# Four graph-attention layers on one core: the row factor G by DMA and ScalarE copies in place of TensorE transposes, with normalisation, statistics and value copies moved between engines

## The chip, the cores and the metric

The kernel runs on one core of one Trainium2 chip. Its time is the device time of one execution in microseconds (us), the median over runs. A core has TensorE (PE, matrix products and transposes), VectorE (DVE), ScalarE (ACT), GpSimd (POOL), and SyncE (SP), which here only issues DMAs. Each engine works through its own queue; semaphores tie the queues together. SBUF is the on-chip memory of 128 partitions, PSUM the memory that TensorE writes.

## The reference

Input x has 16 batches of 1024 nodes with 256 features; one adjacency matrix of 1024 x 1024 serves all. Four layers follow, each `x = x + gat(relu(layernorm(x)))`. A layer has H heads of D = 256/H features, with H = 4, 1, 4, 1:

```python
Wh = h @ W                                  # 1024 x 256, per head 1024 x D
e  = leaky_relu(e_src[i] + e_dst[j])        # slope 0.2, in the last layer 0.01
e  = where(adj[i, j], e, -inf)
y  = softmax(e, over j) @ Wh                # per head
gat = elu(y)                                # in the last layer relu(y)
```

Layers 0 and 1 mask with adj > 0, layers 2 and 3 with adj != 0. `e_src` and `e_dst` are products of Wh with the two halves of the vector a.

## The kernel before

**The algebra.** exp(leaky_relu(s + d)) is the larger of two products of an i-factor and a j-factor. What depends on i alone cancels in the softmax, so that for every pair (j, i) the weight is `w = max(G[i], r[j]) * mask[j, i]`, with the remaining j-factor folded into the values. G[i] is `gcol` (L215, capped in L217), r[j] is `rcol` (L212), and the values `whx` carry the j-factor (L196) in a last column, so that one matrix product gives numerator and denominator.

**Tiling.** The 1024 nodes lie as C = 8 chunks of 128 partitions. A *tile* is the weight matrix of one chunk j against all 1024 i, 128 x 1024 float32 in SBUF, made by one VectorE operation (L236). Its input `g` is G of one head, the same row of 1024 numbers in all partitions, in PSUM. It is made by eight TensorE transposes of a column that is broadcast along the free axis (`broadcast`, L226 to L231); two `g` buffers exist. A four-head layer has 32 tiles, a one-head layer 8.

**Aggregation** (L240 to L256). TensorE multiplies each tile with the values, summing over the eight j. A *group* is what fills one accumulator: in a four-head layer four chunks i of one head (two groups a head), in a one-head layer one chunk i over 257 columns. Each layer has eight groups. ScalarE copies each accumulator to `y` (L256); there are two accumulators.

**Preparation** (L148 to L224). Statistics by VectorE (`stats`, L160, L161), the reciprocal root by GpSimd (L164, L165), the normalised rows by ScalarE (L174), per half of the nodes: four transposes for each 128 features by TensorE (L182), a relu copy by ScalarE (L183), then for each chunk the product with W (L194), an exponential (L196), the copy of the source and destination terms (L198) and the copy of the values: for one head with the factor as scale (L200), for four heads raw (L203), with the factor multiplied in by GpSimd (L205). `factors` ends it.

**Finish** (L258 to L304). Reciprocal of the denominators (L273, VectorE), then for each half a multiplication and a clamp by GpSimd (L277, L282), the exponential of ELU by ScalarE (L286), the combination by VectorE (L292) and the addition to x by GpSimd (L293). After the last layer L295 and the store L296 stand in place of these.

**Order.** 64 *steps* (a batch in a layer) run one after the other, numbered from 0. Four batches are in work at a time, so that a step's preparation and finish can be laid beside the groups of other steps. From step 3 on four-head and one-head steps mostly alternate; in cycles of eight steps the pattern of heads is 4 1 4 1 1 4 1 4. The main loop (L363 to L381) writes the order of all queues out by hand. Each group is a slot. In it stand: the tiles that the group needs; its products and its copy; the pieces of the last step's finish that are due; the pieces of preparations that are due (`prepare`); and some tiles ahead (four in a four-head step, two in a one-head step), no further than WBUFS tiles past what has been consumed. `PREPARATION` gives each piece's slot, counted from the group at which the step is planned: that is group 0 of the step two before, or group 4 where the batch's own last step is too near, as for steps 3, 5, 6, 8, 62 and 63. A tile can be written into the order only once its step's preparation is complete, and `emit_tiles` puts the head's `broadcast` in when the tiles are within half a head of it.

**Buffers.** 21 tiles w, three buffers `t4` shared by normalised rows and exponentials, two PSUM buffers `pp` for transposes and projections.

Of the kernel before, what the change touches and what calls it, by code (L numbers as in the profile page):

```python
# [33 lines left out]
P = 128  # L34
# [4 lines left out]
WBUFS = 21  # L39
PREPARATION = (0, 0, 1, 2, 3, 3, 4, 4, 5, 5, 5, 5, 6, 6, 7, 7, 8)  # L40
# [11 lines left out]
def kernel(ctx: ExitStack, tc: tile.TileContext, x, adj, ws, avs, out):  # L52
# [83 lines left out]
    ps_acc = ctx.enter_context(tc.tile_pool(name="ps_acc", bufs=2, space=PSUM))  # L136
    ps_p = ctx.enter_context(tc.tile_pool(name="ps_p", bufs=2, space=PSUM))
# [10 lines left out]
    def preparation(n):  # L148
# [6 lines left out]
        def stats(half):  # L155
# [6 lines left out]
            if half == 1:  # L162
# [3 lines left out]
                shift = st["shift"] = small.tile([P, C], F32, name="shift")  # L166
                nc.gpsimd.tensor_tensor(shift, st["mv"][:, :, 0], rstd, op=ALU.mult)
                nc.gpsimd.tensor_scalar(shift, shift, -1.0, None, op0=ALU.mult)

        def normalise(half):  # L170
            xn = st["xn", half] = prep.tile([P, HALF, F], F32, name="t4", bufs=3)
            for q in range(HALF):
                c = half * HALF + q
                nc.scalar.activation(xn[:, q, :], xs[b][:, c, :], AF.Identity,  # L174
                                     bias=st["shift"][:, c:c + 1], scale=st["rstd"][:, c:c + 1])
# [10 lines left out]
        def project(c):  # L186
# [12 lines left out]
            if H == 1:  # L199
                nc.scalar.activation(whx[:, c, 0, 0:D], pw[:, 0:D], AF.Copy,  # L200
                                     scale=whx[:, c, 0, D:D + 1])
            else:
                nc.scalar.activation(whx[:, c, :, 0:D],  # L203
                                     pw[:, 0:F].rearrange("p (h d) -> p h d", h=H), AF.Copy)
                nc.gpsimd.tensor_tensor(whx[:, c, :, 0:D], whx[:, c, :, 0:D],  # L205
                                        whx[:, c, :, D:D + 1].to_broadcast([P, H, D]),
                                        op=ALU.mult)
# [10 lines left out]

        out = [lambda: stats(0), lambda: stats(1), lambda: normalise(0), lambda: normalise(1)]
# [3 lines left out]

        return list(zip(PREPARATION, out + [factors], strict=True))  # L224

    def broadcast(n, h):  # L226

        g = state[n]["g", h] = ps_g.tile([P, N], F32, name="g")
        for c in range(C):
            nc.tensor.transpose(g[:, c * P:(c + 1) * P],  # L230
                                state[n]["gcol"][:, c, h:h + 1].to_broadcast([P, P]), ident)  # L231
# [26 lines left out]
    def finish(n):  # L258
# [16 lines left out]
        def scaled(half):  # L275
# [7 lines left out]

        def exponential(half):
# [135 lines left out]
```

## Time and profile before

| | before |
|---|---|
| median of 3 runs | 2823.59 us (2823.42 to 2825.28) |
| the profiled execution | 2825.28 us |
| its span, first to last instruction | 2823.2 us |
| granted TensorE clock, mean | 0.994 |
| busy PE / DVE / ACT / POOL | 2675.6 / 1986.5 / 1054.9 / 897.0 us |
| weight products L252 on PE | 1939.1 us |
| projections L194, transposes of rows L182, G transposes L230 | 509.1, 153.0, 169.6 us |
| tiles L236 on DVE | 1280 of 1273 ns |
| bytes moved by DMA | 45.60 MB |

Busy times are unions over the run; an instruction's own duration overlaps with the start of the next on the same engine, so that a row's sum can exceed what it takes from the queue. The view of the chain follows the last instruction back, at each step to what released it. In the groups, the last column is the idle time of the engine just before the group and what ended most of it. In the order of time the columns are start, duration, engine, line, operation, tiles and count, then the idle time ahead and its releaser. In the view by stretches each pair gives busy time and number of instructions for PE, weight loads (PEld), DVE, ACT and POOL, then the granted clock, the share of the DMA engines and GB/s.

### The profile page before, as it was taken

The page shows a single profiled execution, that of the slowest core. Times are in us where ns is not written, and L with a number is a line of the kernel's source. Part 1 is how long each engine was busy: PE and PEld are TensorE (multiplying, and loading weights), DVE is VectorE, ACT ScalarE, POOL GpSimd, SP SyncE. Part 2 cuts the span into 40 slices and gives each one's busy share as a digit, 9 for nine tenths or more (in the row PEclk, how much of TensorE's full clock was granted, in tenths as well). Part 3 has the DMA queues.
Part 4 walks back from the last instruction along what each step waited for, and adds up shares of the span by engine and source line. Part 5 has one row for each costly group of instructions (what it writes and reads, how often), then busy time and mean ns, then how long its engine had stood idle before and what let it go on. Part 6 is the DMA issues. An engine that isn't in the chain of part 4 may idle for free.

```text
span 2823.2 us, 90054 instructions
## 1 busy us (share of the span) xinstructions
PE 2675.6 (95%) x41296; PEld 2387.0 (85%) x41296; DVE 1986.5 (70%) x2569; ACT 1054.9 (37%) x3041; POOL 897.0 (32%) x909
## 2 busy tenths in 40 slices
PE   1899999999999999999999999999999999999998
PEld 1788888888988888888988889888898888888887
DVE  6597675576975678748777469667696577875672
ACT  0423424343333343343344343343333334344331
POOL 0233424233223244243242243333423324324221
PEclk9999999999999999999999999999999999999999
DMA  4000000000000000000100000000010000000000
GB/s 143 7 3 2 2 2 2 2 32 9 25 32 15 18 2 3 2 1 32 32 2 32 31 2 3 2 2 17 16 33 17 16 32 2 3 2 1 17 17 30
DMA packets 38842, 45.60 MB, mean 16 GB/s; under 512 B 3136, under 2 KB 37440, under 8 KB 38464
## 3 DMA queue, kind: packets, MB, share of 16 engines
q1 hardware_dynamic: 35776, 38.80, 4.1%
q8 instruction: 324, 5.31, 0.8%
q10 hardware_dynamic: 2688, 1.05, 0.1%
q14 instruction: 54, 0.44, 0.1%
HBM read 23.07 MB, written 16.78 MB: 14 GB/s over the span
## 4 chain that ended last, share of the span: by engine, by line
PE 89%; DVE 5%; ACT 3%; DMA 1%; POOL 1%; issue 1%; DVEq 0%; ACTq 0%; SPq 0%; POOLq 0%
PE acc L252 64%; PE pp L194 16%; PE g L230 5%; PE pp L182 4%; DVE w L236 3%; ACT whx L196 1%; ACT whx L200 1%; DMA a_bc<-in_L_gnn_a 1%; ACT y L256 1%; DVE bn L160 0%; ACT whx L203 0%; DVE mask L129 0%; POOL gcol L217 0%; DVE t L292 0%; DVE mv L161 0%
## 5 line engine op out<-in xcount | busy, mean ns | idle before, releaser
L252 PE MATMUL acc<-whx,w 128*64 128x65 f32 x36864 | 1939.1, 241 | 21.7 <-DVE w L236 21.6
L252 PEld LDWEIGHTS acc<-whx,w 128*64 128x64 f32 x36864 | 1749.9, 145 | 180.0 <-issue 41.1
L236 DVE SCALAR_TENSOR_TENSOR w<-g,rcol,mask 128x1024 f32<-128x1024 f32 x1280 | 1544.1, 1273 | 419.7 <-PE acc L252 249.5
L256 ACT ACTIVATE y<-acc 128x260 f32<-128x260 f32 (+1 forms) x512 | 197.8, 386 | 1433.0 <-PE acc L252 1433.0
L194 PE MATMUL pp<-wx,hT 128*128 128x258 f32 (+1 forms) x2048 | 509.1, 392 | 2.0 <-ACT hT L183 2.0
L277 POOL TENSOR_TENSOR y<-y,r 128x1024 f32<-128x1024 f32 x128 | 242.8, 1898 | 814.3 <-DVE r L273 814.3
L194 PEld LDWEIGHTS pp<-wx,hT 128*128 128x128 f32 x2048 | 379.4, 190 | 67.1 <-ACT hT L183 3.0
L205 POOL TENSOR_TENSOR whx<-whx 128x256 f32<-128x256 f32 x256 | 157.7, 617 | 599.0 <-ACT whx L203 599.0
L293 POOL TENSOR_TENSOR x<-x,t 128x1024 f32<-128x1024 f32 x96 | 227.2, 2366 | 227.2 <-DVE t L292 227.2
L174 ACT ACTIVATE t<-x,shift,rstd 128x256 f32<-128x256 f32 x512 | 265.2, 590 | 47.7 <-POOL x L293 42.5
L273 DVE RECIPROCAL r<-y 128x32 f32<-128x32 f32 (+1 forms) x64 | 17.7, 277 | 324.5 <-ACT y L256 324.5
L196 ACT ACTIVATE whx<-pp,nbias 128x4 f32<-128x4 f32 (+1 forms) x512 | 135.3, 264 | 192.0 <-PE pp L194 179.1
L230 PE MATMUL g<-ident,gcol 128*128 128x128 f32 x1280 | 169.6, 275 | 38.8 <-POOL gcol L217 38.8
L160 DVE BATCH_NORM_STATS2 bn<-x 128x6 f32<-128x256 f32 x512 | 200.7, 392 | 2.2 <-DMA x<-in_x 2.2
L230 PEld LDWEIGHTS g<-ident,gcol 128*128 128x128 f32 x1280 | 142.1, 137 | 59.4 <-POOL gcol L217 50.9
L182 PE MATMUL pp<-ident,t 128*128 128x128 f32 x1024 | 153.0, 282 | 27.8 <-ACT t L174 12.7
L182 PEld LDWEIGHTS pp<-ident,t 128*128 128x128 f32 x1024 | 110.9, 141 | 70.5 <-ACT whx L200 28.0
L183 ACT ACTIVATE hT<-pp 128x512 f32<-128x512 f32 x256 | 145.9, 595 | 20.7 <-PE pp L182 19.1
L292 DVE SCALAR_TENSOR_TENSOR t<-t,y 128x1024 f32<-128x1024 f32 x96 | 118.6, 1235 | 39.4 <-ACT t L286 39.4
L200 ACT ACTIVATE whx<-pp,whx 128x256 f32<-128x256 f32 x256 | 121.4, 474 | 0.0
L165 POOL TENSOR_TENSOR rstd<-rstd,neghalf 128x8 f32<-128x8 f32 x64 | 106.7, 1666 | 5.3
L161 DVE BATCH_NORM_AGGREGATE mv<-bn 128x2 f32<-128x6 f32 x512 | 92.8, 181 | 16.9
(35 smaller groups left out, 593.7 us busy)
## 6 DMA issues: line engine op xcount, KB each, us to landing
x<-in_x SPq DMA_DIRECT2D x16, 1024.0 KB, 5.3
out<-x SPq DMA_DIRECT2D x32, 512.0 KB, 3.1
a_raw<-in_adj SPq DMA_DIRECT2D x8, 512.0 KB, 3.7
a_bc<-in_L_gnn_a ACTq DMA_DIRECT2D x8, 128.0 KB, 5.9
wx<-in_L_gnn_W SPq DMA_DIRECT2D x4, 256.0 KB, 12.4
```

The source lines that it names most:

```text
L160: nc.vector.bn_stats(st["bn"][:, c, :], xs[b][:, c, :])
L174: nc.scalar.activation(xn[:, q, :], xs[b][:, c, :], AF.Identity, bias=st["shift"][:, c:c + 1], scale=st["rstd"][:, c:c + 1])
L182: nc.tensor.transpose(pt[:, q, :], st["xn", half][:, q, k * P:(k + 1) * P], ident)
L194: nc.tensor.matmul(pw, lhsT=st["hT", half][:, k, q * P:(q + 1) * P], rhs=wx[l][:, k, :], start=(k == 0), stop=(k == K - 1))
L196: nc.scalar.activation(whx[:, c, :, D], pw[:, F + H:F + 2 * H], AF.Exp, bias=nbias[l], scale=slope)
L205: nc.gpsimd.tensor_tensor(whx[:, c, :, 0:D], whx[:, c, :, 0:D], whx[:, c, :, D:D + 1].to_broadcast([P, H, D]), op=ALU.mult)
L230: nc.tensor.transpose(g[:, c * P:(c + 1) * P], state[n]["gcol"][:, c, h:h + 1].to_broadcast([P, P]), ident)
L236: nc.vector.scalar_tensor_tensor(w, state[n]["g", h], state[n]["rcol"][:, jc, h:h + 1], masks[LAYERS[steps[n][1]][3]][:, jc, :], op0=ALU.m ...
L252: nc.tensor.matmul(acc[o % P:o % P + cols, q, :], lhsT=st["w", h, jc][:, o:o + cols], rhs=st["whx"][:, jc, h, :], start=(jc == 0), stop=(j ...
L256: nc.scalar.activation(st["y"][:, i0:i0 + per, h, :], acc, AF.Copy)
L277: nc.gpsimd.tensor_tensor(yh, yh, r[:, :, None].to_broadcast([P, HALF * H, D]), op=ALU.mult)
L293: nc.gpsimd.tensor_add(xh, xh, e)
```

## The change

G reaches PSUM in another way. At the end of a preparation one transpose turns all of `gcol` into rows (C x H rows of 128), ScalarE copies them to SBUF (`gT`), and a DMA writes them to DRAM, one row of 1024 for each head (`rows`). For each head, `fetch` reads that row from DRAM into all 128 partitions of `gs` (two buffers), and `broadcast` becomes a ScalarE copy from `gs` to PSUM. `fetch_heads` issues fetches up to two heads ahead.

With it: rows are normalised by GpSimd (subtract and multiply in one operation) and not by ScalarE; four-head values are copied head by head by ScalarE with the factor as scale, and the GpSimd multiplication L205 is gone; the exponential of a half stands directly behind its GpSimd operations and no longer a slot later; `prepare` comes after the tiles of a slot; the slots of a preparation are spread from 0 to 10 and not 0 to 8; and there are 19 w buffers.

```diff
@@ -36,8 +36,8 @@
 SHIFT = 60.0
 EXP_SHIFT = math.exp(SHIFT)
 STREAMS = 4
-WBUFS = 21
-PREPARATION = (0, 0, 1, 2, 3, 3, 4, 4, 5, 5, 5, 5, 6, 6, 7, 7, 8)
+WBUFS = 19
+PREPARATION = (0, 1, 1, 1, 3, 3, 4, 4, 5, 5, 6, 6, 7, 7, 8, 8, 9, 10)
 
 
 LAYERS = [
@@ -134,6 +134,7 @@
     work = ctx.enter_context(tc.tile_pool(name="work", bufs=2))
     ps_g = ctx.enter_context(tc.tile_pool(name="ps_g", bufs=2, space=PSUM))
     ps_acc = ctx.enter_context(tc.tile_pool(name="ps_acc", bufs=2, space=PSUM))
+    dram = ctx.enter_context(tc.tile_pool(name="dram", bufs=4, space=bass.MemoryType.DRAM))
     ps_p = ctx.enter_context(tc.tile_pool(name="ps_p", bufs=2, space=PSUM))
 
     L = len(LAYERS)
@@ -163,16 +164,13 @@
                 rstd = st["rstd"] = small.tile([P, C], F32, name="rstd")
                 nc.gpsimd.tensor_scalar(rstd, st["mv"][:, :, 1], EPS, None, op0=ALU.add)
                 nc.gpsimd.tensor_tensor(rstd, rstd, neghalf, op=ALU.pow)
-                shift = st["shift"] = small.tile([P, C], F32, name="shift")
-                nc.gpsimd.tensor_tensor(shift, st["mv"][:, :, 0], rstd, op=ALU.mult)
-                nc.gpsimd.tensor_scalar(shift, shift, -1.0, None, op0=ALU.mult)
 
         def normalise(half):
             xn = st["xn", half] = prep.tile([P, HALF, F], F32, name="t4", bufs=3)
             for q in range(HALF):
                 c = half * HALF + q
-                nc.scalar.activation(xn[:, q, :], xs[b][:, c, :], AF.Identity,
-                                     bias=st["shift"][:, c:c + 1], scale=st["rstd"][:, c:c + 1])
+                nc.gpsimd.tensor_scalar(xn[:, q, :], xs[b][:, c, :], st["mv"][:, c, 0:1],
+                                        st["rstd"][:, c:c + 1], op0=ALU.subtract, op1=ALU.mult)
 
         def transpose(half, k):
             if k == 0:
@@ -196,15 +194,9 @@
             nc.scalar.activation(whx[:, c, :, D], pw[:, F + H:F + 2 * H], AF.Exp, bias=nbias[l],
                                  scale=slope)
             nc.scalar.activation(st["sd"][:, c, :], pw[:, F:F + 2 * H], AF.Copy)
-            if H == 1:
-                nc.scalar.activation(whx[:, c, 0, 0:D], pw[:, 0:D], AF.Copy,
-                                     scale=whx[:, c, 0, D:D + 1])
-            else:
-                nc.scalar.activation(whx[:, c, :, 0:D],
-                                     pw[:, 0:F].rearrange("p (h d) -> p h d", h=H), AF.Copy)
-                nc.gpsimd.tensor_tensor(whx[:, c, :, 0:D], whx[:, c, :, 0:D],
-                                        whx[:, c, :, D:D + 1].to_broadcast([P, H, D]),
-                                        op=ALU.mult)
+            for h in range(H):
+                nc.scalar.activation(whx[:, c, h, 0:D], pw[:, h * D:(h + 1) * D], AF.Copy,
+                                     scale=whx[:, c, h, D:D + 1])
 
         def factors():
             sd = st["sd"]
@@ -216,19 +208,32 @@
                                  scale=-(1.0 - slope))
             nc.gpsimd.tensor_scalar(gcol, gcol, EXP_SHIFT, None, op0=ALU.min)
 
+        def rows():
+
+            pt = ps_p.tile([C * H, P], F32, name="pp")
+            nc.tensor.transpose(pt, st["gcol"].rearrange("p c h -> p (c h)"), ident)
+            gT = small.tile([C * H, P], F32, name="gT", bufs=2)
+            nc.scalar.activation(gT, pt, AF.Copy)
+            st["grow"] = dram.tile([H, C, P], F32, name="grow")
+            nc.sync.dma_start(out=st["grow"].rearrange("h c i -> c h i"), in_=gT)
+
         out = [lambda: stats(0), lambda: stats(1), lambda: normalise(0), lambda: normalise(1)]
         for half in range(2):
             out += [lambda half=half, k=k: transpose(half, k) for k in range(K)]
             out += [lambda c=c: project(c) for c in range(half * HALF, (half + 1) * HALF)]
 
-        return list(zip(PREPARATION, out + [factors], strict=True))
+        return list(zip(PREPARATION, out + [factors, rows], strict=True))
+
+    def fetch(n, h):
+
+        gs = state[n]["gs", h] = work.tile([P, N], F32, name="gs", bufs=2)
+        nc.sync.dma_start(out=gs, in_=state[n]["grow"][h].rearrange("c i -> (c i)")
+                          .partition_broadcast(P))
 
     def broadcast(n, h):
 
         g = state[n]["g", h] = ps_g.tile([P, N], F32, name="g")
-        for c in range(C):
-            nc.tensor.transpose(g[:, c * P:(c + 1) * P],
-                                state[n]["gcol"][:, c, h:h + 1].to_broadcast([P, P]), ident)
+        nc.scalar.activation(g, state[n]["gs", h], AF.Copy)
 
     def weights(n, h, jc):
 
@@ -272,7 +277,7 @@
             st["r"] = small.tile([P, C, H], F32, name="r")
             nc.vector.reciprocal(st["r"], st["y"][:, :, :, D])
 
-        def scaled(half):
+        def exponential(half):
             xh, yh, r = views(half)
             nc.gpsimd.tensor_tensor(yh, yh, r[:, :, None].to_broadcast([P, HALF * H, D]),
                                     op=ALU.mult)
@@ -280,10 +285,7 @@
 
                 e = st["e", half] = prep.tile([P, HALF * H, D], F32, name="t4", bufs=3)
                 nc.gpsimd.tensor_scalar(e, yh, 0.0, -3.0e38, op0=ALU.min, op1=ALU.max)
-
-        def exponential(half):
-            if l < L - 1:
-                nc.scalar.activation(st["e", half], st["e", half], AF.Exp)
+                nc.scalar.activation(e, e, AF.Exp)
 
         def add(half):
             xh, yh, r = views(half)
@@ -299,8 +301,7 @@
             if half == 1 and b + STREAMS < B:
                 load(b + STREAMS)
 
-        return [(0, divide), (0, lambda: scaled(0)), (1, lambda: scaled(1)),
-                (1, lambda: exponential(0)), (2, lambda: exponential(1)),
+        return [(0, divide), (0, lambda: exponential(0)), (1, lambda: exponential(1)),
                 (2, lambda: add(0)), (3, lambda: add(1))]
 
 
@@ -314,7 +315,7 @@
     tiles = [(n, h, jc) for n, (b, l) in enumerate(steps) for h in range(LAYERS[l][0])
              for jc in range(C)]
     place = {t: i for i, t in enumerate(tiles)}
-    done = {"tiles": 0, "g": 0, "free": 0, "prepared": 0, "wanted": 0}
+    done = {"tiles": 0, "g": 0, "gs": 0, "free": 0, "prepared": 0, "wanted": 0}
     agenda = []
 
     def prepare(upto):
@@ -324,11 +325,21 @@
             piece()
             if last:
                 done["prepared"] = n + 1
+                fetch_heads()
 
     def plan(n, at):
         new = preparation(n)
         agenda.extend((at + k, n, piece, i == len(new) - 1) for i, (k, piece) in enumerate(new))
         agenda.sort(key=lambda a: a[:2])
+
+    def fetch_heads():
+
+        while done["gs"] < min(done["g"] + 2 * C, len(tiles)):
+            n, h, _ = tiles[done["gs"]]
+            if n >= done["prepared"]:
+                break
+            fetch(n, h)
+            done["gs"] += C
 
     def emit_tiles(upto, must=False):
         while done["tiles"] < min(upto, len(tiles)):
@@ -343,6 +354,7 @@
                     prepare(-1)
                 broadcast(n, h)
                 done["g"] += C
+                fetch_heads()
             if i >= done["g"]:
                 return
             weights(*tiles[i])
@@ -371,9 +383,9 @@
                     done["free"] = place[n, h, C - 1] + 1
                 while ending and ending[0][0] <= k:
                     ending.pop(0)[1]()
-                prepare(8 * n + k)
                 ahead = 4 if per > 1 else 2
                 emit_tiles(min(done["tiles"] + ahead, done["free"] + WBUFS))
+                prepare(8 * n + k)
             for _, piece in ending:
                 piece()
             ending = finish(n)
```

## The prediction

> **What bounds the kernel now.** I read the page from its top: busy shares, the chain that ended last, the groups.
>
> ```profile
> PE 2675.6 (95%) x41296; PEld 2387.0 (85%) x41296; DVE 1986.5 (70%) x2569; ACT 1054.9 (37%) x3041; POOL 897.0 (32%) x909
> ...
> PE 89%; DVE 5%; ACT 3%; DMA 1%; POOL 1%; issue 1%; DVEq 0%; ACTq 0%; SPq 0%; POOLq 0%
> ...
> L236 DVE SCALAR_TENSOR_TENSOR w<-g,rcol,mask 128x1024 f32<-128x1024 f32 x1280 | 1544.1, 1273 | 419.7 <-PE acc L252 249.5
> ...
> L174 ACT ACTIVATE t<-x,shift,rstd 128x256 f32<-128x256 f32 x512 | 265.2, 590 | 47.7 <-POOL x L293 42.5
> ...
> L230 PE MATMUL g<-ident,gcol 128*128 128x128 f32 x1280 | 169.6, 275 | 38.8 <-POOL gcol L217 38.8
> ```
>
> TensorE carries 89% of the chain; the G transposes are 169.6 us of it. VectorE, at 70%, is second. A mean over the run hides when each limits, so next the busy time in stretches of two steps (84.2 us).
>
> ```profile
> 1202.40:1286.60 84.20, 82.48 (x632) 71.78 (x631) 46.03 (x66) 34.96 (x99) 33.06 (x33) 1.00 0.00 1
> 1286.60:1370.80 84.20, 82.47 (x1291) 73.74 (x1290) 60.80 (x79) 30.84 (x95) 29.24 (x35) 1.00 0.08 27
> 1370.80:1455.00 84.20, 82.48 (x1949) 75.84 (x1949) 75.45 (x91) 31.00 (x92) 22.65 (x25) 1.00 0.09 28
> ```
>
> First TensorE (82.48 in each), then its weight loads, then VectorE: 46 us where two one-head steps meet, 75 us where two four-head steps do. So TensorE bounds everywhere from step 9 on, but VectorE has only 9 us to spare in the third stretch. How near it is shows in VectorE's order of time at the start of a four-head step (TensorE starts head 0 at 1025.24 and head 2 at 1043.39):
>
> ```profile
> 1020.52 2.48 DVE L236 SCALAR_TENSOR_TENSOR w<-g,rcol,mask 128x1024 f32<-128x1024 f32 x2 [12.68 <-PE acc L252]
> 1023.99 0.20 DVE L273 RECIPROCAL r<-y 128x8 f32<-128x8 f32 x1 [0.98 <-ACT y L256]
> 1028.32 9.60 DVE L236 SCALAR_TENSOR_TENSOR w<-g,rcol,mask 128x1024 f32<-128x1024 f32 x8
> 1037.83 1.21 DVE L292 SCALAR_TENSOR_TENSOR t<-t,y 128x1024 f32<-128x1024 f32 x1
> 1038.96 4.86 DVE L236 SCALAR_TENSOR_TENSOR w<-g,rcol,mask 128x1024 f32<-128x1024 f32 x4
> ```
>
> 13 tiles of the step are made ahead, 12 more by 1043.7, so tile 23, which head 2 needs within 0.8 us, is there 1.5 us early. A tile is 1.20 us apart from the next; between 1024.1 and 1028.3 lie the statistics (2.07 us a half).
>
> **What the Trainium skill says.** "PSUM — Partial Sum Buffer", section "Engine vs sequencer instructions": ScalarE, VectorE and GpSimd queues are strict FIFO; so the order of emission decides, and the trace agrees (the reciprocal waits 0.98 us and nothing passes it). "SBUF — State Buffer", section "SBUF: two separate sides": VectorE with two SBUF inputs and GpSimd lock each other out for a whole instruction. L236 has one SBUF tensor (g is in PSUM) and keeps its 1.27 us; the last two L295 took 4.03 us beside a running L277, so it can bite. "DMA: Bandwidth & Descriptors", section "Anatomy of one DMA — SWDGE (gpsimd) path": about 2 us fixed, mostly the write's receipt; our 512 KB store lands in 3.1 us.
>
> **The change part by part.** Steps of four heads and of one head alternate, in cycles of eight: 4 1 4 1 1 4 1 4. I cost a cycle (336.8 us before), then the start and the end.
>
> *Removed from TensorE.* A head's eight transposes put its next group off by 1.02 us in a four-head step (1032.86 to 1033.88) and 0.87 in a one-head step (996.66 to 997.53): 20 heads, 19.2 us. The wait for gcol ahead of a step's first transpose (38.8 us over 32, 1.2 each): 4 in a cycle, 4.9. The second half's transposes (L182) no longer stand straight behind two projections whose PSUM buffers ScalarE has yet to free (1.35 us for eight against 0.95): 8 x 0.4 = 3.2. Added: one transpose of gcol a step, two instructions of 0.14: 8 x 0.3 = 2.4. Net -24.9.
>
> *VectorE's lead.* The new order has rows at slot 10 of a preparation, not factors at 8, statistics after the tiles of a group, and 19 w buffers. In a one-head step only slots 3 to 7 then make tiles of the next step, two each: 10, not 13, ahead of the reciprocal. With 0 at TensorE's start of the step: reciprocal done -1.1; tiles 10-13 to 3.7; half the statistics 5.8; tiles 14-17 10.6; other half 12.7; residual op 13.7; tiles 18-21 18.5; residual op 19.6; tile 23 at 22.0. TensorE is at head 2 after four groups (3.81 each), one pair of projections (2.0), rows 0.3 and half a step's transposes 0.95: 18.5, plus 0.8 to tile 23: 19.3. It waits 2.7 us. A four-head step behind a four-head step starts VectorE 1.4 us later: 4.1. Per cycle 3 x 2.7 + 4.1 = +12.2. Later heads and the next step's tiles come in time.
>
> *The way of G.* Transpose, ScalarE copy, 16 KB to DRAM, 512 KB back to 128 partitions, ScalarE copy to PSUM. In four-head steps it is early by several groups, which hide it. In a one-head step rows end at 12.5, gT 13.0, store 14.8 (1.8: below the 3.1 of 512 KB, near the skill's fixed 2), fetch 4.2 more, copy 1.05 (L286: 1048 ns for 1024 elements): G in PSUM at 20.2. The trace has no fetch of one row to all partitions. The same bytes from 128 rows take 3.7 (a_raw); 1 MB (x) takes 5.3, and two heads are fetched together; a repeated source could be slower (a_bc, 128 KB: 5.9 with its queue full). I take 4.2, ends 3.5 and 7. Queued behind that copy on ScalarE is the first half's relu (hT), and TensorE's projection, due at 20.4, waits for it: hT at 21.3, so 0.9 us, 4 times a cycle: +3.6.
>
> *ScalarE and GpSimd.* ScalarE loses 512 normalising ops of 590 ns and gains 160 copies of 1.05 and 768 short copies (by the fit of L198, L203 and the operand's extra from L200 some 0.3 us, overlapping): its share stays near 40%. GpSimd loses L205 (158 us) and shift, gains 512 x 0.44 us (between L217's 0.29 for 32 elements and L282's 1.06 for 1024) = 225. Its first half ends at about 15.5 in a one-head step, transposes start at 16.0: hidden with 0.5 to spare; if an op took 0.6 it would show. The second half reuses the first's buffer and so waits for TensorE's transposes, with the residual adds behind it; they have until the next step. Exponentials directly behind GpSimd's two ops: their input is there at 2.2, ScalarE is at them at 4.3: nothing.
>
> A cycle: -24.9 + 12.2 + 3.6 = -9.1; 51 steps (9 to 59) are 6.4 cycles: -58.
>
> *Start and end.* Steps 3, 5, 6, 8, 62 and 63 are planned at group 4, so rows now fall at slot 6 of the step just before. From rows: 7.6 us to G, 9.6 for eight tiles; what is left to cover them is a group and a projection. One-head steps wait some 7 to 9, four-head steps 10. Carried from step to step with the durations above against the times before: step 9 starts at 536, not 523.3 (+13: 37 us of new waits, less G's transposes, less VectorE-bound waits that TensorE already had); the end +13.5 (step 61 +0.7, 62 +7.3, 63 +5.5).
>
> Sum: -58 + 13 + 13.5 = -31 against the profiled 2825.28 (span 2823.2): 2794; the median of the runs is 2823.59, so I say 2793. This kernel's runs tell 0.2% (6 us) from no change.
>
> **Rivals.** *The fetch is slow* (slower than before). Each us of it beyond 4.2 costs 26 us in the one-head steps and 6 in the late ones: 32. At 5.2 the gain is gone; at 7, 2883. For it: a repeated source row, two heads together, a store in front. Against: the engines' share is 0.09 at most in the stretches above. *GpSimd is in the way*: normalising at 0.6 us an op holds the first half's transposes by 0.3 us, or its lock delays L292 by 1 to 1.9: some 1 us in 30 of the steps, 2823: no change. *VectorE is never late* (it drifts ahead in one-head steps): 78 us of waits vanish, 2715. Against: the reciprocal fences it off once a step. ScalarE as the bound I rule out at 40%.
>
> **How the numbers follow.** Forecast 0.45 (fetch 3.5 to 4.9, 2771 to 2815); slow fetch 0.30 (2828 to 2890); GpSimd 0.15 (2810 to 2845); no lateness 0.10. Faster: 0.45 less a little, plus the last, 0.52; same 0.08; slower 0.40. The range 2750 to 2880 leaves out the fastest case and fetches of 7 us and more; the likeliest case alone has 2771 to 2815.
>
> **What would show it.** L230's group gone from TensorE; w waits of some 2.7 us at head 2 of four-head steps; in the third group of one-head steps ScalarE waiting for gs; gs landing at 3.5 to 4.9 us; tiles waiting at steps 3, 5, 6, 8, 62, 63. Wrong if gs lands after 5.2, if transposes wait for normalising, or if PE waits for w elsewhere.

## The result and the profile after

The changed kernel takes 2913.11 us (2904.84 to 2916.8), the kernel before 2823.63 us (2823.42 to 2825.28): a ratio of 1.031, 95% interval 1.029 to 1.034. The forecast was 2793, its range 2750 to 2880. The profiled execution has a span of 2907.9 us against 2823.2, and the mean granted TensorE clock is 0.964 against 0.994.

From the page of the kernel after: busy shares, the chain that ended last, and the groups that matter (busy time and mean ns of one, then idle time of the engine ahead of the group and its releaser).

```profile
PE 2642.2 (91%) x40080; PEld 2315.1 (80%) x40080; DVE 1992.7 (69%) x2569; ACT 1095.9 (38%) x3521; POOL 1376.2 (47%) x1037
...
PE 59%; DVE 18%; POOL 16%; ACT 3%; DMA 2%; issue 2%; DVEq 0%; SPq 0%; POOLq 0%; ACTq 0%
...
L257 PE MATMUL acc<-whx,w 128*64 128x65 f32 x36864 | 2013.5, 245 | 47.0 <-DVE w L241 47.0
...
L172 POOL TENSOR_SCALAR t<-x,mv,rstd 128x256 f32<-128x256 f32 x512 | 627.2, 1237 | 65.0 <-PE pp L180 58.2
...
L180 PE MATMUL pp<-ident,t 128*128 128x128 f32 x1024 | 183.0, 296 | 153.6 <-POOL t L172 150.0
...
L236 ACT ACTIVATE g<-gs 128x1024 f32<-128x1024 f32 x160 | 163.8, 1024 | 70.8 <-DMA gs<-grow 70.8
```

GpSimd holds 16% of the chain where it held 1%. The normalising op (L172) takes 1237 ns, not the 0.44 us that I had given it, and TensorE waits 150.0 us ahead of the transposes that need its rows. The weight products L257 are the same 36,864 instructions as L252 before, yet take 2013.5 us in place of 1939.1. ScalarE waits 70.8 us for fetched rows; whether TensorE feels that is taken up under "The way of G" and "Start and end" below.

The same three stretches as in the prediction, with the same columns:

```profile
1202.40:1286.60 84.20, 79.76 (x1074) 70.66 (x1070) 54.60 (x79) 33.30 (x109) 46.47 (x34) 0.98 0.04 14
1286.60:1370.80 84.20, 79.65 (x1240) 70.59 (x1239) 59.90 (x77) 30.68 (x97) 39.47 (x30) 0.96 0.18 59
1370.80:1455.00 84.20, 79.73 (x1357) 71.06 (x1355) 64.34 (x69) 33.83 (x115) 38.93 (x30) 0.98 0.24 78
```

TensorE is busy for 79.7 us of 84.2, not 82.5, though less work was left to it, and the clock, third from the end, is 0.96 to 0.98 and not 1.00. DMA moves more, and stays below a quarter of its engines' time.

Where in the run the 84.7 us of span went is read from the 64 reciprocals, one for each step, in both traces. Up to that of step 8 the kernel after loses 34.9 us (*start*), over the next 50 steps 25.3 (*middle*, 6.25 cycles), after that 24.5 (*end*). The forecast had +13, -58 and +13.5.

What a loss in the middle looks like, in the order of time of GpSimd and then of TensorE, in a one-head step that TensorE begins at 1022.88:

```profile
1033.65 0.91 POOL L209 TENSOR_SCALAR gcol<-gcol 128x32 f32<-128x32 f32 x1 [5.64 <-ACT gcol L207]
1034.64 0.25 POOL L165 TENSOR_SCALAR rstd<-mv 128x8 f32<-128x8 f32 x1
1034.97 1.67 POOL L166 TENSOR_TENSOR rstd<-rstd,neghalf 128x8 f32<-128x8 f32 x1
1036.74 4.84 POOL L172 TENSOR_SCALAR t<-x,mv,rstd 128x256 f32<-128x256 f32 x4
```

```profile
1035.21 3.64 PE L257 MATMUL acc<-whx,w 128*128 128x257 f32 x16
1038.69 0.27 PE L180 MATMUL pp<-ident,t 128*128 128x128 f32 x1
1039.24 0.33 PE L180 MATMUL pp<-ident,t 128*128 128x128 f32 x1 [0.28 <-POOL t L172]
1040.44 0.33 PE L180 MATMUL pp<-ident,t 128*128 128x128 f32 x1 [0.87 <-POOL t L172]
1041.64 0.83 PE L180 MATMUL pp<-ident,t 128*128 128x128 f32 x5 [0.87 <-POOL t L172]
1042.27 5.30 PE L257 MATMUL acc<-whx,w 128*128 128x257 f32 x16
```

GpSimd waits 5.64 us for `gcol` of one step while the reciprocal root of the next stands behind it in its queue. It then normalises from 13.9 us after the step's start to 18.7. The transposes are due at 15.8 and trickle, one per op of GpSimd. And the group behind them takes 5.30 us, where the same 16 instructions ahead of them took 3.64. Why is seen in slices of 2 us (clock third from the end):

```profile
1037.50:1039.50 2.00, 1.72 (x9) 1.11 (x7) 0.00 (x0) 0.38 (x1) 2.00 (x3) 1.00 0.39 104
1039.50:1041.50 2.00, 0.40 (x2) 0.14 (x1) 0.00 (x0) 0.00 (x0) 2.00 (x2) 1.00 1.00 289
1041.50:1043.50 2.00, 1.86 (x8) 1.65 (x9) 0.54 (x1) 1.60 (x3) 0.94 (x2) 0.68 0.32 131
1043.50:1045.50 2.00, 2.00 (x6) 1.58 (x5) 2.00 (x3) 0.43 (x1) 2.00 (x3) 0.50 0.66 217
1045.50:1047.50 2.00, 2.00 (x10) 1.72 (x10) 2.00 (x2) 0.00 (x0) 2.00 (x3) 0.97 0.12 49
```

After two slices in which TensorE was partly idle (busy for 0.40 of 2.00 us in the second) the granted clock falls to 0.50. Cut at the moments where it falls and comes back, the same place reads:

```profile
1038.80:1042.21 3.41, 1.39 (x9) 0.85 (x8) 0.00 (x0) 0.70 (x2) 2.79 (x3) 1.00 0.92 290
1042.21:1045.62 3.41, 3.41 (x10) 2.76 (x9) 2.66 (x3) 1.72 (x3) 2.97 (x3) 0.50 0.42 142
```

The Trainium skill, "TensorE: Matmul & The Clock Gate", section "Part 1: The HAM clock gate (the "warmup" mystery)", says that an idle window of about 3.4 us halves TensorE's clock until it has been busy for as long; this trace agrees in the half and in the length, 3.41 us. But TensorE was not idle in the window ahead, it was busy for 1.39 of 3.41 us, and the measurement decides.

In the middle of the run the clock stands at 0.50 in 27 stretches (25 of 3.41 us, two of 6.83), one in each of 27 of the 50 steps. Their starts lie whole multiples of one length, 3.413 us, apart. In the 3.41 us ahead of each of them TensorE was busy for 0.94 to 1.70 us, at most half; of the 594 other stretches of this grid in the middle, only one (1.67 us) was as idle. So it depends on where a stall falls on the grid whether it costs clock: steps in which TensorE is idle for 2.02 us in all are there with the drop (7 of them) and without it (5).

Where the drop comes, the stall is paid twice, as a wait and as slower work after it. The group above lies in the slow stretch for 3.35 us and loses 5.30 - 3.64 = 1.66 us, half of that. Taking this half for all such stretches gives the estimates of the clock's cost below: TensorE's busy time in stretches at 0.50, halved. In the middle of the kernel after it is 48.1 us, in the kernel before nothing.

### The profile page after: what moved, and what is told of

Same layout as the page of the kernel before. It is cut to its first block, busy times and chain, and to the rows that moved or that the text cites. A ratio compares the mean times of both kernels' runs of the same rounds, so it can differ in the third digit from the quotient of the medians.

```text
span 2907.9 us, 89029 instructions
## 1 busy us (share of the span) xinstructions
PE 2642.2 (91%) x40080; PEld 2315.1 (80%) x40080; DVE 1992.7 (69%) x2569; ACT 1095.9 (38%) x3521; POOL 1376.2 (47%) x1037
## 4 chain that ended last, share of the span: by engine, by line
PE 59%; DVE 18%; POOL 16%; ACT 3%; DMA 2%; issue 2%; DVEq 0%; SPq 0%; POOLq 0%; ACTq 0%
PE acc L257 42%; DVE w L241 12%; PE pp L192 12%; POOL t L172 10%; PE pp L180 4%; POOL rstd L166 3%; DVE bn L161 3%; DVE mv L162 1%; POOL rstd L165 1%; DMA gs<-grow 1%; ACT t L288 1%; POOL gcol L209 1%; ACT y L261 1%; DMA a_bc<-in_L_gnn_a 0%; ACT g L236 0%
## 5 line engine op out<-in xcount | busy, mean ns | idle before, releaser
L257 PE MATMUL acc<-whx,w 128*64 128x65 f32 x36864 | 2013.5, 245 | 47.0 <-DVE w L241 47.0
L257 PEld LDWEIGHTS acc<-whx,w 128*64 128x64 f32 x36864 | 1800.0, 148 | 248.0 <-DVE w L241 70.9
L172 POOL TENSOR_SCALAR t<-x,mv,rstd 128x256 f32<-128x256 f32 x512 | 627.2, 1237 | 65.0 <-PE pp L180 58.2
L282 POOL TENSOR_TENSOR y<-y,r 128x1024 f32<-128x1024 f32 x128 | 242.2, 1897 | 810.7 <-DVE r L278 810.7
L198 ACT ACTIVATE whx<-pp,whx 128x64 f32<-128x64 f32 (+1 forms) x1280 | 358.8, 347 | 0.0
L180 PE MATMUL pp<-ident,t 128*128 128x128 f32 x1024 | 183.0, 296 | 153.6 <-POOL t L172 150.0
L180 PEld LDWEIGHTS pp<-ident,t 128*128 128x128 f32 x1024 | 121.3, 144 | 204.0 <-POOL t L172 189.6
L209 POOL TENSOR_SCALAR gcol<-gcol 128x32 f32<-128x32 f32 (+1 forms) x64 | 33.3, 520 | 436.0 <-ACT gcol L207 435.9
L294 DVE SCALAR_TENSOR_TENSOR t<-t,y 128x1024 f32<-128x1024 f32 x96 | 121.8, 1268 | 164.5 <-ACT t L288 164.4
L236 ACT ACTIVATE g<-gs 128x1024 f32<-128x1024 f32 x160 | 163.8, 1024 | 70.8 <-DMA gs<-grow 70.8
L165 POOL TENSOR_SCALAR rstd<-mv 128x8 f32<-128x8 f32 x64 | 39.1, 610 | 156.8 <-DVE mv L162 154.5
L287 POOL TENSOR_SCALAR t<-y 128x1024 f32<-128x1024 f32 x96 | 103.2, 1075 | 9.0
```

Source lines behind the costliest of these rows:

```text
L172: nc.gpsimd.tensor_scalar(xn[:, q, :], xs[b][:, c, :], st["mv"][:, c, 0:1], st["rstd"][:, c:c + 1], op0=ALU.subtract, op1=ALU.mult)
L180: nc.tensor.transpose(pt[:, q, :], st["xn", half][:, q, k * P:(k + 1) * P], ident)
L198: nc.scalar.activation(whx[:, c, h, 0:D], pw[:, h * D:(h + 1) * D], AF.Copy, scale=whx[:, c, h, D:D + 1])
L236: nc.scalar.activation(g, state[n]["gs", h], AF.Copy)
L257: nc.tensor.matmul(acc[o % P:o % P + cols, q, :], lhsT=st["w", h, jc][:, o:o + cols], rhs=st["whx"][:, jc, h, :], start=(jc == 0), stop=(j ...
L282: nc.gpsimd.tensor_tensor(yh, yh, r[:, :, None].to_broadcast([P, HALF * H, D]), op=ALU.mult)
```

## The experiments

All times stand against the kernel before. *Start*, *middle* and *end* are measured as above, in one profiled execution each.

| run | median us | ratio (95% interval) | start | middle | end |
|---|---|---|---|---|---|
| after | 2913.1 | 1.0312 (1.0286 to 1.0337) | +34.9 | +25.3 | +24.5 |
| e1_scalar_norm | 3078.0 | 1.0894 (1.0867 to 1.0922) | +49.2 | +163.1 | +28.3 |
| e2_before_gpsimd_norm | 2840.4 | 1.0061 (1.0046 to 1.0076) | +13.2 | +1.4 | 0.0 |
| e3_plan_alone | 2878.5 | 1.0196 (1.0179 to 1.0213) | +22.6 | +22.9 | +6.8 |
| e4_op_forms | 2854.8 | one run | +37.2 | -32.8 | +25.3 |
| e5_stats_early | 2830.0 | 1.0020 (1.0010 to 1.0030) | +42.1 | -60.6 | +23.0 |
| e6_late_list | 2814.6 | 0.9966 (0.9955 to 0.9978) | +40.5 | -62.5 | +9.3 |
| e7_g_transposed | 2779.5 | 0.9845 (0.9828 to 0.9861) | +3.4 | -54.3 | +4.1 |
| e8_undo_dma | 2919.8 | 1.0346 (1.0329 to 1.0363) | +0.6 | +81.1 | +10.1 |
| e9_late_by_transposes | 2811.0 | 0.9951 (0.9936 to 0.9966) | +25.5 | -62.2 | +19.3 |
| e10_more_tiles | 2779.4 | 0.9840 (0.9826 to 0.9855) | +5.6 | -54.7 | +4.1 |
| e11_ends_by_transposes | 2804.5 | 0.9933 (0.9919 to 0.9946) | +24.6 | -61.4 | +15.8 |
| e12_no_empty_slot | 2772.3 | 0.9817 (0.9804 to 0.9830) | +3.0 | -62.1 | +6.9 |

### Normalising: the engine and its op

**e1_scalar_norm**, from the kernel after:

```diff
-                nc.gpsimd.tensor_scalar(xn[:, q, :], xs[b][:, c, :], st["mv"][:, c, 0:1],
-                                        st["rstd"][:, c:c + 1], op0=ALU.subtract, op1=ALU.mult)
+                nc.scalar.activation(xn[:, q, :], xs[b][:, c, :], AF.Identity,
+                                     bias=st["shift"][:, c:c + 1], scale=st["rstd"][:, c:c + 1])
```

(The two GpSimd operations that make `shift` come back as well.)

> The kernel after, with the rows normalised by ScalarE again (bias and scale, as in the kernel before); G by DMA, the order, the slots and all else stay. Theory: the GpSimd normalising at 1237 ns an op is what cost the forecast; then TensorE no longer waits for L172 (150 us before the transposes) and the time falls to about the forecast, 2793 (2771 to 2830), with waits for w at head 2 of four-head steps now in sight. Rival (the way of G and the late start of tiles cost it, and normalising merely hid them): the transposes' wait is replaced by waits for w or hT, and the time stays above 2860.

My theory in this form fell: 3078 us, 165 worse than the kernel after. In ScalarE's waits:

```profile
ACT t L175 <- POOL shift L169: 275.9, 60, 10.0
```

The second half of the statistics stands a slot later in the order than in the kernel before, so `shift` does, and ScalarE stands still for it 275.9 us (three columns: sum, times, longest), with the copies of `hT`, `gT` and the accumulators behind it in its queue. TensorE then waits 141.4 us behind `gT` and 73.0 for `hT`. So the run brings in a wait of its own and cannot say what the 1237 ns cost. It shows that within this order ScalarE normalises worse than GpSimd.

**e2_before_gpsimd_norm**: the same two lines exchanged the other way in the kernel before, and the two operations for `shift` left out.

> The kernel before, with only the normalising moved to GpSimd. Theory: the op takes about 1.2 us here too; a half takes 5 us, GpSimd has L205 to do besides, and TensorE waits 1 to 4 us ahead of the first transposes of a step: 2850 to 2980. Rival (1237 ns comes of what else the kernel after does, and normalising alone is hidden): an op at 0.4 to 0.6 us, the time within 10 us of 2823.

The op takes 1.22 us as its median here too (its line L171), yet the middle is +1.4 and the time, 2840.4, is below my range: neither theory as it was put, since I expected it to show. In TensorE's waits it stands four times, all in the first preparation, 13.3 us of it at once:

```profile
PE pp L179 <- POOL t L171: 15.5, 4, 13.3
```

With the slots of the kernel before GpSimd starts early enough, and even 1.2 us an op is hidden.

**e3_plan_alone**, from the kernel before:

```diff
-WBUFS = 21
-PREPARATION = (0, 0, 1, 2, 3, 3, 4, 4, 5, 5, 5, 5, 6, 6, 7, 7, 8)
+WBUFS = 19
+PREPARATION = (0, 1, 1, 1, 3, 3, 4, 4, 5, 5, 6, 6, 7, 7, 8, 8, 9)
...
-                prepare(8 * n + k)
                 ahead = 4 if per > 1 else 2
                 emit_tiles(min(done["tiles"] + ahead, done["free"] + WBUFS))
+                prepare(8 * n + k)
```

> The kernel before, with only the new order: prepare after the tiles of a slot, slots 0 to 9 (the list of the kernel after without its rows), 19 w buffers; G by transposes, normalising by ScalarE. Theory as in the forecast: VectorE's lead shrinks, four-head steps wait some 1 to 3 us for w at head 2, steps planned late wait more: 2840 to 2900. Rival (VectorE is never late): within 6 us of 2823, apart from the steps planned late, at most 2840.

The time is in the range, the mechanism isn't mine. Of TensorE's waits:

```profile
PE acc L252 <- ACT y L256: 71.8, 53, 1.8
PE acc L252 <- DVE w L236: 28.0, 40, 2.8
```

In the middle TensorE never waits for w, but 65.3 us for accumulators that ScalarE has not yet copied, since it waits 278.2 us for `shift` as in e1. Whether VectorE would be late behind that, this run cannot show.

**e4_op_forms**, from the kernel after, the four ops of a half in four forms: two immediates, one column, a second tensor, and two columns as it was:

```diff
-                nc.gpsimd.tensor_scalar(xn[:, q, :], xs[b][:, c, :], st["mv"][:, c, 0:1],
-                                        st["rstd"][:, c:c + 1], op0=ALU.subtract, op1=ALU.mult)
+                if q == 0:
+                    nc.gpsimd.tensor_scalar(xn[:, q, :], xs[b][:, c, :], 0.0, 0.5,
+                                            op0=ALU.subtract, op1=ALU.mult)
+                elif q == 1:
+                    nc.gpsimd.tensor_scalar(xn[:, q, :], xs[b][:, c, :], st["rstd"][:, c:c + 1],
+                                            None, op0=ALU.mult)
+                elif q == 2:
+                    nc.gpsimd.tensor_tensor(xn[:, q, :], xs[b][:, c, :],
+                                            st["rstd"][:, c:c + 1].to_broadcast([P, F]),
+                                            op=ALU.mult)
+                else:
+                    nc.gpsimd.tensor_scalar(xn[:, q, :], xs[b][:, c, :], st["mv"][:, c, 0:1],
+                                            st["rstd"][:, c:c + 1], op0=ALU.subtract, op1=ALU.mult)
```

> The kernel after, with the four normalising ops of a half in four forms on GpSimd, each on its own line: two immediates, one scalar read from a column, a tensor_tensor with the column broadcast along the row, and the form as it is with two columns. The rows of three of them are not normalised (the mean is not taken off, or neither factor is applied), so the values differ from the reference. Theory: the scalars read from columns are what is slow: immediates near 0.3 to 0.45 us, one column 0.7 to 0.8, two columns 1.24. Rival (256 elements cost 1.2 us in any form, or it is contention with VectorE): all four within 0.9 to 1.3 us.

Each line's own view (ns: least, median, greatest):

```profile
L173 POOL TENSOR_SCALAR t<-x x128: 1067/1081/1362, 65.9 to 2753.6; 128x256 f32<-128x256 f32 x128
L176 POOL TENSOR_SCALAR t<-x,rstd x128: 923/932/937, 71.8 to 2754.7; 128x256 f32<-128x256 f32 x128
L179 POOL TENSOR_TENSOR t<-x,rstd x128: 610/615/622, 72.7 to 2755.6; 128x256 f32<-128x256 f32 x128
L183 POOL TENSOR_SCALAR t<-x,mv,rstd x128: 1227/1235/2324, 73.3 to 2756.2; 128x256 f32<-128x256 f32 x128
```

The rival is nearer: columns add only 0.15 us. It is the arithmetic of a tensor_scalar that is slow: subtract and multiply on 256 elements take as long as the min and max of L287 on 1024 (1075 ns on the page), from which I had priced them. Multiplying with a second tensor takes 0.6. A half here takes 3.86 us, 1.0 less than the 4.88 of the kernel after, and the middle is 58.1 us shorter, 1.16 us a step: 26.3 us of it less idle time of TensorE (84.3 against 110.6), and 31.7 less busy time, which is as much as the clock accounts for (10 stretches at 0.50 and not 27, an estimate of 16.5 us against 48.1). This is one execution, and the clock's share depends on how the stalls fall on the grid.

### When GpSimd begins, and the way of G

**e5_stats_early**, from the kernel after, one number:

```diff
-PREPARATION = (0, 1, 1, 1, 3, 3, 4, 4, 5, 5, 6, 6, 7, 7, 8, 8, 9, 10)
+PREPARATION = (0, 0, 1, 1, 3, 3, 4, 4, 5, 5, 6, 6, 7, 7, 8, 8, 9, 10)
```

> The kernel after with one number changed in the list of slots: the second half of the statistics stands at slot 0 and not at slot 1, so that GpSimd can begin to normalise a slot earlier; its op still takes 1.24 us. Theory (what costs the steady part is when GpSimd starts on the rows, which hides VectorE's lateness behind it): the waits of TensorE for L172 fall from 150 us to under 40, waits for w at head 2 of four-head steps come into sight at 1 to 3 us, the steady part of 51 steps gains 30 to 86 us, the start and the end stay: 2825 to 2885. Rival (GpSimd is simply short of time in a step, wherever it starts): the wait stays above 100 us and the time above 2895.

2830: 83 us from one number, with the same op. The reciprocal root now comes ahead of `gcol` in GpSimd's queue, and the middle is -60.6, close to the forecast (-58), in part by luck: less work left TensorE than I had taken, and it also waited less (see "Removed from TensorE" and "VectorE's lead" below). All of TensorE's waits in it, e5 and then the kernel after:

```profile
PE acc L257 <- DVE w L241: 38.6, 38, 1.6
PE pp L214 <- POOL gcol L209: 20.9, 15, 1.4
PE pp L180 <- POOL t L172: 9.8, 38, 0.3
PE pp L192 <- ACT hT L181: 2.7, 3, 0.9
```

```profile
PE pp L180 <- POOL t L172: 110.6, 148, 1.2
```

The wait that VectorE's lateness was to bring is there once GpSimd's is gone.

**e7_g_transposed**: e5 without `rows`, `fetch` and the ScalarE copy of g, with the eight transposes (L226 to L231 of the kernel before) in `broadcast` and slots that end with the factors at 9.

> As the run with early statistics, but G by eight transposes a head as in the kernel before (no rows, fetches or ScalarE copies of G). Theory (TensorE is the bound and sheds 24.9 us a cycle by the DMA way, of which late tiles and fetches give some back): 9 to 25 us more a cycle in the steady part, that is 60 to 160, and up to 25 less in the start and the end: 40 to 140 above the run with early statistics. Rival (VectorE sets the pace in this order and every us that TensorE sheds is waited for again): within 20 us of that run.

It is 50 us *faster* than e5: the theory had the sign wrong. In the middle G by DMA is worth 6.3 us (-60.6 against -54.3), and it costs 38.7 in the start and 18.9 in the end.

**e8_undo_dma**: e7 with the statistics' second half at slot 1, so that against the kernel after only the way of G is undone.

> The kernel after with only G's way undone: eight transposes a head as before, no rows, fetches or ScalarE copies of G; statistics, GpSimd's normalising, slots (0 to 9), order and 19 w buffers as in the kernel after. Theory (the way of G by DMA costs some 57 us in the start and the end and gives 6 back in the middle; the late start of GpSimd costs its 83 us apart from that): about 50 less than the kernel after, 2835 to 2885, the wait for L172 still above 80. Rival (the time that the transposes of G take hides the normalising, so that the two parts only cost together): 2770 to 2800.

2919.8, outside the range: the two parts don't add. With GpSimd late, G by DMA is worth 55.8 us in the middle, and that pays for what it costs at both ends. The middle of the five kernels, in us, idle being the length less TensorE's busy time:

| statistics' second half; G | length | PE busy | PE idle | clock |
|---|---|---|---|---|
| kernel before | 2102.3 | 2058.8 | 43.5 | 1.00 |
| slot 1; DMA (after) | 2127.5 | 2016.9 | 110.6 | 0.98 |
| slot 0; DMA (e5) | 2041.7 | 1969.6 | 72.1 | 1.00 |
| slot 1; transposes (e8) | 2183.4 | 2102.6 | 80.8 | 0.98 |
| slot 0; transposes (e7) | 2047.9 | 2043.6 | 4.4 | 1.00 |

After and e5 run the same instructions; of the 47.4 us between their busy times the slower clock is some 40 (estimated as above: 48.1 against 7.9), and between e8 and e7 some 44 of 59.0 (44.4 against nothing). What the rest is, no run separates. Without the transposes TensorE's busy time falls by 74.0 (e7 to e5), but its idle time rises by 67.7: the tiles begin a slot later and VectorE has nothing in hand (38.6), and `rows` waits for `gcol` (20.9).

### Start and end

**e6_late_list**, from e5: steps planned at group 4 use a second list.

```diff
+LATE = (0, 0, 0, 1, 3, 3, 4, 4, 5, 5, 5, 5, 6, 6, 7, 7, 7, 8)
-        return list(zip(PREPARATION, out + [factors, rows], strict=True))
+        return list(zip(LATE if n and ready_at[n] >= n - 3 else PREPARATION, out + [factors, rows], strict=True))
```

> As the run with early statistics, and besides the six steps that are planned at group 4 have a shorter list of slots (statistics and the first half's normalising at 0, rows at 8 and not at 10). Theory (the start and the end lose because a late-planned step's G comes too late): 20 to 45 us less than the run with early statistics, the steady part the same. Rival (the start and the end lose because of how long the normalising takes or of the fetches, not of the slot of rows): less than 10 us between the two.

15.4 us less by the medians, between theory and rival: 13.7 in the end, 1.6 in the start. In the start the w waits fell from 49.0 us to 24.4. But `rows`, now close behind the factors, made TensorE wait for `gcol`, 23.6 us against 4.8 and up to 6.6 at once. And it waits 14.4 us (1.1 in e5) ahead of row transposes that now stand straight behind two projections. In the longest such wait, 5.70 us at 222.10, ScalarE has yet to free the PSUM buffers and itself waits 4.45 us for GpSimd at an exponential.

**e9_late_by_transposes**: e5 with G by transposes in steps 0 to 2 and those planned late. **e11_ends_by_transposes**: in all of steps 0 to 8 and 60 to 63. The core of e11 (in e9 the condition is `n < 3 or ready_at[n] >= n - 3`; in both `broadcast` has both ways and `fetch_heads` leaves such heads out):

```diff
+    def by_transposes(n):
+        return n < 9 or n >= 60
...
         def rows():
+            if by_transposes(n):
+                return
```

> As the run with early statistics (2830), but G goes by TensorE transposes in the steps 0 to 2 and in the six that are planned at group 4 (3, 5, 6, 8, 62, 63), and by DMA in all others. Theory (in these steps alone the way by DRAM is on the path): the start and the end come to what the run with transposes everywhere has, within 15 us, the middle to what the run with early statistics has: 2765 to 2795. Rival (start and end lose by something else that comes with the DMA way, such as DMA traffic or the copies on ScalarE, or step 4, 7 and 61 lose as well): 2805 or more.

> As the run with early statistics, but G by transposes in all of steps 0 to 8 and 60 to 63 (so in 4, 7, 60 and 61 too, which are not planned late), by DMA in steps 9 to 59. Theory (what the start and the end still lost, 22 and 15 us, is the way of G in the steps between the late ones): start and end as with transposes everywhere (+3 and +4 against the kernel before), the middle as with early statistics (-60): 2770 to 2780. Rival (it is something else that the DMA way brings in, such as the order of rows and slots or the slower clock after the waits): 2790 or more.

Both missed: the start stayed at +25, the end at +16 to +19. In e11 these steps had no DMA of G left, but still the empty last piece at slot 10. A step's tiles may be written into the order only when its last piece is done, so they still began one slot later than in e7.

**e12_no_empty_slot**, from e11:

```diff
+        if by_transposes(n):
+            return list(zip(PREPARATION[:-1], out + [factors], strict=True))
```

> As the run with transposes in steps 0 to 8 and 60 to 63, in which the last slot of their preparations, 10, was left as an empty piece, so that their tiles could be written into the order one slot later than with transposes everywhere (a step counts as prepared with its last piece). Here their list ends with the factors at slot 9. Theory (that one slot, not the DMA, is what start and end still lost): start +3 and end +4 against the kernel before, the middle -60, so 2765 to 2778, and faster than the run with transposes everywhere (2779.5). Rival (something else of the DMA way): 2795 to 2806, no change.

Start +3.0, end +6.9, middle -62.1. So of the 39 us that the start lost by the way of G, 21.6 are that slot (e11 to e12) and 17.5 the way itself (e5 to e11); in the end 8.9 and 7.2. At 2772.3 us it is the fastest kernel of the study, 1.8% below the kernel before.

**e10_more_tiles**: e7 with 21 w buffers.

> As the run with G by transposes and early statistics (2779), with 21 w buffers and not 19. Theory (TensorE waits for w there only in the start, 27 us in all, at the pace of VectorE): within 6 us of it. Rival (19 buffers hold VectorE back throughout): 10 to 40 us less.

No change (2779.4): with G by transposes the loss of two buffers costs nothing. With G by DMA no run tells.

## Why the prediction was wrong, step by step

**The step that failed: "gains 512 x 0.44 us".** The op takes 1.237. Where GpSimd begins and when TensorE wants its rows were right: its first half was to end "at about 15.5", transposes to start at 16.0, and measured in the step above are 18.7 and 15.8. The 0.44 was read off the min operations L217 and L282, of 32 and of 1024 elements: sizes on both sides of the 256, and the wrong operation (e4). The page of the kernel before had a multiplication of the right size, and it was over the 0.6 us at which I said that it would show:

```profile
L205 POOL TENSOR_TENSOR whx<-whx 128x256 f32<-128x256 f32 x256 | 157.7, 617 | 599.0 <-ACT whx L203 599.0
```

I had named the rival, but bounded it at 0.6 us, when no row showed subtract and multiply at this size. With 1.237 the same sum gives 2.7 us in each of 51 steps, 138, which hides the 78 of VectorE's waits and the 23 of fetches: -58 + 138 - 78 - 23 = -21 in the middle. Without the slower clock (48.1, estimated) the middle measured 25.3 - 48.1 = -22.8. That the two agree so well is luck: the waits were 110.6 us and not 138, and TensorE shed less than the forecast took off.

**The term that was missing: the clock.** No part of the sum has it. By the estimate above it cost 15.4 us more than in the kernel before in the start, 48.1 in the middle and 13.0 in the end, 76.5 of the 84.7 us of span. Measured beside it, L257's same instructions take 74.4 us more over the whole run, and in e7, whose clock never falls in the middle, only 9.0 more (1948.1).

**Removed from TensorE, -24.9 a cycle: the size about right, the cause half wrong.** In e5 busy time falls by 89.2, 14.3 a cycle (16.8 forecast, and 17.4 by the forecast's own durations, since 16 x 1.02 and 4 x 0.87 make 19.8 for the transposes of G and not 19.2), and the waits for `gcol` and for PSUM buffers by 43.6, 7.0 a cycle (8.1). But e7, which keeps the transposes of G, loses those waits too, and so does e3 in the middle, which has only the new order, the slots and 19 buffers: it is the order that removes them, not the DMA. A wait that I had not seen came in, `rows` for `gcol`, 3.3 a cycle.

**VectorE's lead, +12.2: right place, half the size, and hidden.** e5 waits 6.2 a cycle for w. Of its 38.6 us in the middle 34.4 stand at the start of head 2 of four-head steps, as forecast, and 4.2 at head 1. In the kernel after the wait at the transposes, straight ahead of it, takes it in: there TensorE never waits for w in the middle.

**The way of G, +3.6: right in time, almost nothing on the path in the middle.** In the step shown above the fetch was issued at 1037.71, 1.85 us after the store, and ScalarE's copy began at 1041.90: 4.2 us, as taken, and 1024 ns for the copy. In the 33 places where ScalarE waits for a fetch, it is 3.46 to 4.88 us from the issue to the copy, so the slow fetch, my main rival, did not occur. The 1.8 us for the store lean on a section of the Trainium skill that is on DMAs issued by GpSimd, as its title says; this one is issued by SyncE, and took 1.85. In e5 `hT` is late by 0.4 us a cycle. ScalarE, at 38%, bounds nothing here.

**Start and end, +13 and +13.5: right waits, without the clock.** They are 34.9 and 24.5. The waits stand where they were forecast, at the first tile of steps 5, 6, 8, 62 and 63 (2.2 to 4.4 us, then shorter ones tile by tile at VectorE's pace). The last of them, step 63, shows the way of G on the path, from the fetch over the copy and the tile to the product:

```profile
2857.28 0.33 SPq L230 DMA_DIRECT2D gs<-grow  x1
2860.97 1.03 ACT L236 ACTIVATE g<-gs 128x1024 f32<-128x1024 f32 x1 [1.54 <-DMA gs<-grow]
2862.03 7.24 DVE L241 SCALAR_TENSOR_TENSOR w<-g,rcol,mask 128x1024 f32<-128x1024 f32 x6 [26.71 <-ACT g L236]
2863.37 4.80 PE L257 MATMUL acc<-whx,w 128*128 128x257 f32 x8 [4.36 <-DVE w L241]
```

In the end TensorE is idle for 13.6 us more than in the kernel before, and busy for 11.0 more although the transposes of 7 heads are gone; the clock there is 0.91 and not 0.98 (some 13.0 us by the estimate). In the start it is idle for 37.5 us more. Its busy time should have fallen by some 26 us (27 heads in steps 0 to 8, 0.95 each) and fell by 2.5; the slower clock (0.94 against 0.97) is some 15.4 of the difference. And I had counted the later slot as a part of G's latency, when in the runs from e5 on it alone is worth more (21.6 us of the start, against 17.5 for the way itself).

## What to carry to other kernels

Price an op on GpSimd from a row with the same operation, not the same size, and if there is none let the range reach to several times the guess. An op that moves to another engine is judged by when that engine can begin it: one slot in the order of GpSimd's queue was worth 83 us here, the op's cost unchanged. And count a stall of TensorE with the slower clock behind it: where TensorE stood still for half of a stretch of 3.41 us or more, a stretch at half the clock could follow, that is some 1.7 us lost.

## What was new of the hardware

- GpSimd on 128x256 float32: tensor_scalar with subtract and multiply 1081 ns by immediates, 1235 by columns, multiply alone 932, tensor_tensor multiply 615; min and max on 128x1024 take 1075 (L287 of the kernel after).
- The granted clock falls to 0.50 without TensorE being idle for a whole window: in the middle of the kernel after 27 stretches at 0.50 start on one grid of 3.41 us, each behind 3.41 us in which TensorE was busy for 0.94 to 1.70 us. A group of 3.64 us then takes 5.30. The line is near half, but not sharp in the busy time of the profile: in e8 26 stretches stand behind 1.46 to 1.83 us, and five others as idle have none behind them.
- Fetching one row of 4 KB from DRAM into all 128 partitions took 3.46 to 4.88 us from issue to use (33 fetches), where the 512 KB of a_raw from as many rows as partitions took 3.7 from issue to landing.
- GpSimd's op on `gcol` took 0.91 us in the step shown and at most 0.29 in the kernel before. VectorE's residual op L294 (its inputs t and y both in SBUF) ran from 1033.18 to 1034.41, and the GpSimd op began at 1033.65 and ended at 1034.56. That fits the shared lock of the Trainium skill's "SBUF — State Buffer", section "SBUF: two separate sides"; no run isolates it.
